# Grouped 5x5 convolutions on TensorE: from sixteen 32x32 tiles to eight 64x32 tiles, with the image rows read back from DRAM

## The chip, the cores and the metric

The kernel runs on one core of a Trainium2 chip. The core has TensorE (PE, matrix products), VectorE (DVE), ScalarE (ACT), GpSimd (POOL) and SyncE (SP); DMAs are issued by SP and POOL. The metric is the time of one execution on the device in microseconds, and lower is better. All numbers are f32.

## The reference, cut to what matters

The input is 4 images of 512 channels and 64x64 pixels. The first layer is a linear attention. It projects the image to queries, keys and values; a second set of them comes from a 5x5 depthwise convolution of the first set, followed by a pointwise convolution inside groups of 8 channels:

```python
qkv = concat(h @ wq.T, h @ wk.T, h @ wv.T)                        # 3 x 512 channels
dw  = conv(qkv, dw_kernel, 5x5, SAME, feature_group_count=3*512)  # each channel by itself
pw  = conv(dw, pw_kernel, 1x1, feature_group_count=3*64)          # 8 channels to 8
f   = concat(qkv, pw)                                             # 128 heads of 8
query, key = relu(...), relu(...)
scores = einsum("bhdn,bhen->bhde", value_with_ones, key)
out = einsum("bhde,bhen->bhdn", scores, query); out = out[:-1] / (out[-1:] + 1e-15)
x = batchnorm(conv1x1(out)) + x
```

The second layer computes four edge maps from the result (3x3 stencils), takes them through 1x1 convolutions, a channel attention, a fusing product with a layer norm, and adds the input.

## The kernel before, in words

The kernel computes the two convolutions of keys and queries (5x5 by channel, then 8 to 8) as one. The weights `mat` are made on POOL as products of the depthwise and pointwise weights (`load_mat`, L242 to L252, loaded as `dp_sb`). For values the kernel does not convolve; it correlates turned keys with shifted values instead (`correlate`, L457).

The 512 channels of each image are worked on in 4 groups of 128, so 16 groups in all. An image of 64 rows is cut into eight strips of 8 rows: strip j = (half, k) has the rows 32 half + k + 4 n, so every fourth row. `project` (L268) makes one strip of keys or queries: four matmuls of 128x128 weights and 512 columns, a copy to `strip` on ACT (L277), and then four DMAs from POOL (L283), each with 32 channels. They put the strip into a kept tile `inps[t]` of four row phases: partition 4 c + r holds channel c and the rows with phase r, so that 32 partitions are 8 channels by 4 rows.

`convolve` (L402) contracts those 32 partitions: 8 channels and 4 neighbouring rows at once. Its 32 output columns are 4 rows by 8 channels. Since 4 output rows need 8 input rows, each output takes two blocks `b` of four rows, and five column shifts `dx`. There are 16 tiles of 32x32 (four row quadrants i, four column quadrants j), so 5 x 2 x 16 = 160 matmuls into four PSUM banks. ACT copies the banks out with a relu (L415 for keys, L421 for queries).

What PE does is an order written out by hand. `keys_and_values` (L563 and on) projects a group's keys and values, strip by strip, and between them does the end of the group before: its queries' convolutions, divisions and foldings. `queries` projects the queries and convolves the keys. After the first image, the later layers of the image before (`stages`: `project_out` L661, `edge_branches` L738, `fuse_out` L850) lie between these steps: `run` and `advance` give them a share of the time after every step, by planned times such as `T_CONV`. The other engines and the SP queue are ordered by a scheduler, with priorities in the order of the program.

SP issues nearly all loads and stores: x (L259), weights (L240), the value strips `vt` to DRAM (L303) and back as `near` (L442), the divided heads and cheads (L390, L559), and for the later layers `hd` (L643, L645), `xr` (L658), `win`, `yr` and `ef`. POOL issues the strips (L283), `y` (L670) and `ef` (L751).

Of the kernel before, what the change touches and what calls it, by code (L numbers as in the profile page):

```python
# [8 lines left out]
F32 = mybir.dt.float32  # L9
# [65 lines left out]

LEFT_E = 14.0

T_PROJ, T_TURN, T_SCORES, T_CONV, T_CORR, T_SMALL = 3.4, 0.5, 0.3, 10.6, 1.1, 0.9


WORK, VALS = 18, 3
# [8 lines left out]
def conv_seq_kernel(  # L90
# [13 lines left out]
    gw = front.enter_context(tc.tile_pool(name="gw", bufs=2))  # L104
    vals = front.enter_context(tc.tile_pool(name="vals", bufs=VALS))
    work = front.enter_context(tc.tile_pool(name="work", bufs=WORK))
    ctx.enter_context(tc.manual_schedule(engines={mybir.EngineType.PE}))

    def work_tile(name, n=512):
# [12 lines left out]
    def rows(ap, width=W):  # L122
        return ap.rearrange("p (r c) -> p r c", c=width)
# [18 lines left out]
    nc.gpsimd.memset(ones, 1.0)  # L142


    inps = {}
    for t in (KEY, QUERY):
        inps[t] = keep.tile([P, 4, NB, W], F32, name=f"inp{t}")
        nc.gpsimd.memset(inps[t][:, :, 0, :], 0.0)
        nc.gpsimd.memset(inps[t][:, :, NB - 1, :], 0.0)

    vts = []
    for n in range(3):
# [73 lines left out]
    class Group:  # L226


        def __init__(self, b, heads, cheads, folded, g):
            self.b, self.heads, self.cheads, self.folded, self.g = b, heads, cheads, folded, g  # L230
            self.near_dram = near[(NG * b + g) % 2]
            self.w, self.mat = {}, {}
            self.strip, self.rq, self.held, self.conv, self.near = {}, {}, {}, {}, {}
            self.nears = iter([(half, jp, b) for half in range(2) for jp in range(2) for b in range(2)])


# [4 lines left out]

        def load_mat(self, t):  # L242

            dp = gw.tile([P, 4, 48], F32, name="dp_sb", tag="dp_sb", bufs=2)
            nc.sync.dma_start(out=dp, in_=dpk[self.g, t // QUERY])
            self.mat[t] = gw.tile([P, 4, 40, 8], F32, name="mat", tag="mat")
            nc.gpsimd.tensor_tensor(
                self.mat[t],
                dp[:, :, 0:40].unsqueeze(3).to_broadcast([P, 4, 40, 8]),
                dp[:, :, 40:48].unsqueeze(2).to_broadcast([P, 4, 40, 8]),  # L250
                ALU.mult,
            )  # L252

# [8 lines left out]
        def project(self, t, j):  # L262
            half, k = STRIPS[j]
            if (self.b, j) not in xs:
                self.load_x(j)
            ps = ps_tile("proj")
            for c in range(NCH):
                nc.tensor.matmul(  # L268
                    ps, lhsT=self.w[t][:, c, :], rhs=xs[self.b, j][c], start=(c == 0), stop=(c == NCH - 1)
                )  # L270
# [6 lines left out]
            nc.scalar.copy(s, ps)  # L277
            if t == KEY:
                self.strip[j] = s

            r, b = (k + 2) % 4, 8 * half + (k + 2) // 4
            for n in range(4):
                nc.gpsimd.dma_start(out=inps[t][r::4, n, b : b + 8, :], in_=rows(s)[32 * n : 32 * n + 32, :, :])  # L283

        def values(self, j):
            half, k = STRIPS[j]
# [106 lines left out]

        def convolve(self, t, half):
            banks = quad_tiles("cv")
            last = len(DXS) * 2 - 1
            for n, (dx, b) in enumerate((dx, b) for dx in DXS for b in range(2)):
                c0, c1 = _span(dx, W)
                for j in range(4):
                    for i in range(4):  # L400
                        q = slice(32 * i, 32 * i + 32)
                        nc.tensor.matmul(  # L402
                            rows(banks[i])[32 * j : 32 * j + 32, :, c0:c1],
                            lhsT=self.mat[t][q, j, (dx + 2) * 8 + 4 * b : (dx + 2) * 8 + 4 * b + 4, :],
                            rhs=inps[t][q, j, 8 * half + b : 8 * half + b + 8, c0 + dx : c1 + dx],
                            start=(n == 0), stop=(n == last),
                        )
# [155 lines left out]
        def keys_and_values(self, before):  # L563
# [16 lines left out]
            def co(jp, first):  # L580
# [5 lines left out]
                q("convolve", QUERY, 0), pj(KEY, 4), q("mix"), q("conv_weights"), sc(2), tr(3), pj(VALUE, 4),  # L586
                q("conv_heads"), q("conv_denominators", 0), pj(KEY, 5), q("conv_fold"), sc(3), tr(4), q("conv_divide", 0),
                pj(VALUE, 5), q("convolve", QUERY, 1), pj(KEY, 6), sc(4), tr(5), pj(VALUE, 6), q("conv_denominators", 1),
                [(0.0, self.load_wtab)], pj(KEY, 7), sc(5), tr(6), q("conv_divide", 1), pj(VALUE, 7),
                [(0.0, lambda: self.load_near(VALS))],  # L590
            ], [])

        def queries(self):


            def pj(j):
                return [(T_PROJ, lambda: self.project(QUERY, Q_ORDER[j]))]
# [366 lines left out]
    for n, cur in enumerate(groups):  # L964
        cur.load_mat(KEY)
        cur.load_w(QUERY)
        if n < 2:
            near_border(near[n])
        run(cur.keys_and_values(groups[n - 1] if n else None))
        if n and n % NG == 0:  # L970
            last = groups[n - 1]
# [152 lines left out]
```

## Time and profile before

| | |
|---|---|
| three runs | 4884.3, 4897.24, 4912.68 us; median 4897.24 |
| profiled execution | span 4886.7 us, from the first to the last instruction; no other time of it is given; clock granted to PE 0.979 |
| PE | 4653.5 us busy (95%) |
| DVE, ACT, POOL | 2103.5, 1593.8, 1113.0 us busy (43%, 33%, 23%) |
| DMA | 864.11 MB, 177 GB/s; the queue of SP 49.0%, that of POOL 9.0% of 16 engines' time |

The profile has a row for each group of equal instructions: source line, engine, operation, output and inputs, shape, count, then after a bar the busy time in us and the mean of one in ns, and after another bar the engine's idle time just before them with what ended most of it. An f32 matmul gives two records, each with a weight load. Matmuls are pipelined, so the mean of one record (600 ns) is longer than the time by which the next follows; busy time counts overlapping records once. Views of a single stretch list an engine's instructions in order of time, merged where they are alike.

### The profile page before, as it was taken

What the parts mean: (1) busy time and instruction counts of PE and PEld (TensorE: products, weight loads), DVE (VectorE), ACT (ScalarE), POOL (GpSimd) and SP (SyncE); (2) the same over time, 40 slices, a digit from 0 to 9 for tenths busy, and PEclk for the clock granted to TensorE, in tenths of its full rate; (3) what the DMA queues carried; (4) which work ended last, traced back from release to release, by engine and by line L of the source; (5) the groups of instructions that cost most, each with busy time, mean ns of one, the idle gap of its engine ahead of it and who ended that gap; (6) DMA issues with size and microseconds to landing.
All of it is one profiled execution on the core that took longest, in us unless ns stands there. A gap on an engine that the chain in (4) does not pass through costs nothing. (4 is left out here: it accounts for less than half of the span.)

```text
span 4886.7 us, 107506 instructions
## 1 busy us (share of the span) xinstructions
PE 4653.5 (95%) x46140; PEld 2698.7 (55%) x46140; DVE 2103.5 (43%) x2788; ACT 1593.8 (33%) x2725; POOL 1113.0 (23%) x1535
## 2 busy tenths in 40 slices
PE   9999999999999999999999999989999999799987
PEld 5666655455666565454565666445446566444433
DVE  1222222114555635311365553441125666447966
ACT  2121111002454524300244452430013545214765
POOL 3122212111221214311212121431111211011443
PEclk9999999999999999999999999999999999899998
DMA  6444456665665666766565666666556555564445
GB/s 205 133 129 134 135 191 188 163 173 162 205 185 188 196 204 202 223 181 161 175 189 191 183 201 186 203 200 192 152 169 184 184 181 185 160 166 148 152 144 170
DMA packets 469227, 864.11 MB, mean 177 GB/s; under 512 B 193000, under 2 KB 225800, under 8 KB 450320
## 3 DMA queue, kind: packets, MB, share of 16 engines
q1 hardware_dynamic: 415760, 721.90, 49.0%
q0 software_dynamic: 52992, 135.35, 9.0%
q8 instruction: 363, 5.95, 0.5%
q14 instruction: 112, 0.92, 0.1%
HBM read 575.93 MB, written 213.98 MB: 162 GB/s over the span
## 5 line engine op out<-in xcount | busy, mean ns | idle before, releaser
L268 PE MATMUL proj<-xt,w_sb 128*128 128x512 f32 x2048 | 942.3, 603 | 32.3 <-DMA xt<-in_x 27.5
L661 PE MATMUL yps<-hd,fold_sb 128*128 128x512 f32 x2048 | 903.5, 597 | 14.7 <-DMA hd<-heads 13.2
L283 POOL DMA_DIRECT2D inp<-strip x1024 | 546.4, 536 | 1345.4 <-ACT strip L277 1314.2
L402 PE MATMUL cv<-inp,mat 32*32 32x512 f32 (+1 forms) x20480 | 738.7, 600 | 60.0 <-issue 43.1
L661 PEld LDWEIGHTS yps<-hd,fold_sb 128*128 128x128 f32 x2048 | 385.5, 191 | 504.2 <-issue 463.8
L268 PEld LDWEIGHTS proj<-xt,w_sb 128*128 128x128 f32 x2048 | 377.9, 192 | 513.4 <-issue 450.8
L402 PEld LDWEIGHTS cv<-inp,mat 32*32 32x32 f32 x20480 | 448.3, 104 | 319.0 <-issue 160.8
L850 PE MATMUL zps<-ef,wf_sb 128*128 128x512 f32 (+1 forms) x1056 | 470.3, 599 | 29.6 <-ACT z L855 15.7
L290 PEld LDWEIGHTS val<-w_sb,xt 128*128 128x128 f32 x4096 | 471.1, 192 | 42.0 <-issue 32.8
L290 PE MATMUL val<-w_sb,xt 128*128 128x128 f32 x4096 | 486.6, 277 | 0.0
L738 PE MATMUL br<-maps,wbr_sb 128*128 128x256 f32 (+1 forms) x1792 | 464.7, 412 | 0.6 <-issue 0.4
L666 DVE SCALAR_TENSOR_TENSOR yt<-yps,shift,xr 128x512 f32<-128x512 f32 x128 | 96.0, 750 | 820.4 <-PE yps L661 790.4
L738 PEld LDWEIGHTS br<-maps,wbr_sb 128*128 128x128 f32 x1792 | 335.2, 190 | 138.2 <-issue 97.3
L277 ACT COPY strip<-proj 128x512 f32<-128x512 f32 x256 | 148.9, 582 | 653.8 <-PE proj L268 653.8
L850 PEld LDWEIGHTS zps<-ef,wf_sb 128*128 128x128 f32 x1056 | 204.1, 197 | 273.6 <-issue 230.3
L457 PE MATMUL corr<-near,ckt 128*32 128x160 f32 x8192 | 330.9, 314 | 21.3 <-DMA near<-near 21.3
L714 DVE TENSOR_TENSOR maps<-dv 128x1054 f32<-128x1054 f32 (+1 forms) x112 | 159.6, 1425 | 396.4 <-PE br L738 396.3
L670 POOL DMA_DIRECT2D y<-yt x128 | 114.7, 896 | 945.4 <-DVE yt L666 772.2
L457 PEld LDWEIGHTS corr<-near,ckt 128*32 128x32 f32 x8192 | 255.3, 111 | 115.9 <-issue 60.0
L881 POOL TENSOR_TENSOR z<-z,yr 128x512 f32<-128x512 f32 (+1 forms) x132 | 174.9, 1343 | 223.0 <-ACT z L878 125.2
L751 POOL DMA_DIRECT2D ef<-ef_o x112 | 81.8, 730 | 613.6 <-ACT ef_o L746 587.6
L318 ACT ACTIVATE kt<-tr 128x512 f32<-128x512 f32 x128 | 76.1, 595 | 438.5 <-PE tr L316 437.9
(131 smaller groups left out, 4373.3 us busy)
## 6 DMA issues: line engine op xcount, KB each, us to landing
xt<-in_x SPq DMA_DIRECT2D x316, 512.0 KB
near<-near SPq DMA_DIRECT2D x512, 264.0 KB
inp<-strip POOLq DMA_DIRECT2D x1024, 64.0 KB, 3.7
win<-y SPq DMA_DIRECT2D x96, 396.0 KB
near<-vt SPq DMA_DIRECT2D x512, 66.0 KB
y<-yt POOLq DMA_DIRECT2D x128, 264.0 KB, 6.3
heads<-q SPq DMA_DIRECT2D x128, 256.0 KB
cheads<-cq SPq DMA_DIRECT2D x128, 256.0 KB
```

The source lines that it names most:

```text
L268: nc.tensor.matmul(ps, lhsT=self.w[t][:, c, :], rhs=xs[self.b, j][c], start=(c == 0), stop=(c == NCH - 1))
L277: nc.scalar.copy(s, ps)
L283: nc.gpsimd.dma_start(out=inps[t][r::4, n, b : b + 8, :], in_=rows(s)[32 * n : 32 * n + 32, :, :])
L290: nc.tensor.matmul(ps[:, ts(c, P)], lhsT=xs[self.b, j][n][:, ts(c, P)], rhs=self.w[VALUE][:, n, :], start=(n == 0), stop=(n == NCH - 1),)
L402: nc.tensor.matmul(rows(banks[i])[32 * j : 32 * j + 32, :, c0:c1], lhsT=self.mat[t][q, j, (dx + 2) * 8 + 4 * b : (dx + 2) * 8 + 4 * b + 4, :],
L457: nc.tensor.matmul(self.banks[jj][32 * i : 32 * i + 32, 160 * b : 160 * b + 160], lhsT=self.held["c", i][:, at : at + 32], rhs=v[:, 4 * n ...
L661: nc.tensor.matmul(ps, lhsT=fold_sb[g // NG][:, g % NG, ts(c, P)], rhs=hd[g], start=(g == 0), stop=(g == 2 * NG - 1),)
L670: nc.gpsimd.dma_start(out=y[c, :, at : at + 29 : 4, :], in_=yt)
L714: nc.vector.tensor_sub(flat[:, half : 3 * half - 2], dvs[:, 2 : 2 * half], dvs[:, 0 : 2 * half - 2])
L738: nc.tensor.matmul(rows(ps), lhsT=wbr_sb[:, k, c, :], rhs=rows(maps[:, slot[k], c % 2, :], WB)[:, :, 0:W], start=(c == 0), stop=(c == NCH ...
L850: nc.tensor.matmul(ps, lhsT=wf_sb[:, k, ts(c, P)], rhs=ef[k], start=(k == 0), stop=(k == 3))
L881: nc.gpsimd.tensor_add(rows(z), rows(z), rows(yr, WB)[:, :, 1 : W + 1])
```

## The change

The kept tiles `inps` go. Each strip is stored whole, by one POOL DMA, into a DRAM tile `flat` (phase, channel, row, column; two of them for keys and two for queries, used in turn by the groups). Its two border rows are zeroed once. A new method `roll` reads one half of the image back, by eight SP DMAs, into a tile `rolled` whose partition 8 c + r holds channel c and eight neighbouring rows r of each block of four. Every row is read twice, as one of the first four and as one of the last four. 64 partitions are now 8 channels by 8 rows, so a convolution contracts all rows an output needs at once and has no `b` any more: 5 shifts x 2 sets s x 4 column quadrants j x 2 row halves i = 80 matmuls on 64x32 tiles. Set s = 0 fills the first two banks, set s = 1 the other two. Weights are laid out anew for that, with as many elements. The rolls of the keys are issued at the end of `keys_and_values`, those of the queries at the end of `queries`. The planned `T_CONV` changes from 10.6 to 9.2.

```diff
-T_PROJ, T_TURN, T_SCORES, T_CONV, T_CORR, T_SMALL = 3.4, 0.5, 0.3, 10.6, 1.1, 0.9
+T_PROJ, T_TURN, T_SCORES, T_CONV, T_CORR, T_SMALL = 3.4, 0.5, 0.3, 9.2, 1.1, 0.9
...
+    rolled = front.enter_context(tc.tile_pool(name="rolled", bufs=2))
...
-    inps = {}
-    for t in (KEY, QUERY):
-        inps[t] = keep.tile([P, 4, NB, W], F32, name=f"inp{t}")
-        nc.gpsimd.memset(inps[t][:, :, 0, :], 0.0)
-        nc.gpsimd.memset(inps[t][:, :, NB - 1, :], 0.0)
+    flats = {
+        (t, n): dram.tile([4, P, NB, W], F32, name=f"flat{t}{n}", bufs=1) for t in (KEY, QUERY) for n in range(2)
+    }
+    def flat_border(n):
+        for t in (KEY, QUERY):
+            for r in range(4):
+                nc.gpsimd.dma_start(out=flats[t, n][r, :, 0 if r < 2 else NB - 1, :], in_=zero_row[:, 0, 0:W])
...
-            for n in range(4):
-                nc.gpsimd.dma_start(out=inps[t][r::4, n, b : b + 8, :], in_=rows(s)[32 * n : 32 * n + 32, :, :])
+            nc.gpsimd.dma_start(out=self.flat[t][r, :, b : b + 8, :], in_=rows(s))
+        def roll(self, t, half):
+            self.rolled[t, half] = rolled.tile([P, 8, 512], F32, name="rolled", tag="rolled")
+            for r in range(8):
+                at = 8 * half + r // 4
+                nc.sync.dma_start(
+                    out=self.rolled[t, half][r::8, :, :],
+                    in_=self.flat[t][r % 4, :, at : at + 8, :].rearrange("(n c) b w -> c n (b w)", c=16),
+                )
...
         def convolve(self, t, half):
             banks = quad_tiles("cv")
-            last = len(DXS) * 2 - 1
-            for n, (dx, b) in enumerate((dx, b) for dx in DXS for b in range(2)):
-                c0, c1 = _span(dx, W)
-                for j in range(4):
-                    for i in range(4):
-                        q = slice(32 * i, 32 * i + 32)
-                        nc.tensor.matmul(
-                            rows(banks[i])[32 * j : 32 * j + 32, :, c0:c1],
-                            lhsT=self.mat[t][q, j, (dx + 2) * 8 + 4 * b : (dx + 2) * 8 + 4 * b + 4, :],
-                            rhs=inps[t][q, j, 8 * half + b : 8 * half + b + 8, c0 + dx : c1 + dx],
-                            start=(n == 0), stop=(n == last),
-                        )
+            image = self.rolled.pop((t, half))
+            for s in range(2):
+                for n, dx in enumerate(DXS):
+                    c0, c1 = _span(dx, W)
+                    for j in range(4):
+                        for i in range(2):
+                            q = slice(64 * i, 64 * i + 64)
+                            nc.tensor.matmul(
+                                rows(banks[2 * s + i])[32 * j : 32 * j + 32, :, c0:c1],
+                                lhsT=self.mat[t][q, 4 * s + j, (dx + 2) * 4 : (dx + 2) * 4 + 4, :],
+                                rhs=rows(image[q, 2 * j + s, :])[:, :, c0 + dx : c1 + dx],
+                                start=(n == 0), stop=(n == len(DXS) - 1),
+                            )
...
# keys_and_values:
-                [(0.0, self.load_wtab)], pj(KEY, 7), sc(5), tr(6), q("conv_divide", 1), pj(VALUE, 7),
-                [(0.0, lambda: self.load_near(VALS))],
+                [(0.0, self.load_wtab)], pj(KEY, 7), sc(5), tr(6), [(0.0, lambda: self.roll(KEY, 0))],
+                q("conv_divide", 1), pj(VALUE, 7),
+                [(0.0, lambda: self.load_near(VALS)), (0.0, lambda: self.roll(KEY, 1))],
...
# queries:
-                ct(1, 3), own("denominators", 0),
+                [(0.0, lambda: self.roll(QUERY, 0)), (0.0, lambda: self.roll(QUERY, 1))], ct(1, 3), own("denominators", 0),
```

More of the change, by code (lines that the diff above doesn't have):

```diff
@@ L232, in __init__ @@
             self.w, self.mat = {}, {}
-            self.strip, self.rq, self.held, self.conv, self.near = {}, {}, {}, {}, {}
+            self.strip, self.rq, self.held, self.conv, self.near, self.rolled = {}, {}, {}, {}, {}, {}
+            self.flat = {t: flats[t, (NG * b + g) % 2] for t in (KEY, QUERY)}
             self.nears = iter([(half, jp, b) for half in range(2) for jp in range(2) for b in range(2)])
@@ L242, in load_mat @@
         def load_mat(self, t):
-            dp = gw.tile([P, 4, 48], F32, name="dp_sb", tag="dp_sb", bufs=2)
+            dp = gw.tile([P, 8, 28], F32, name="dp_sb", tag="dp_sb", bufs=2)
             nc.sync.dma_start(out=dp, in_=dpk[self.g, t // QUERY])
-            self.mat[t] = gw.tile([P, 4, 40, 8], F32, name="mat", tag="mat")
+            self.mat[t] = gw.tile([P, 8, 20, 8], F32, name="mat", tag="mat")
             nc.gpsimd.tensor_tensor(
                 self.mat[t],
-                dp[:, :, 0:40].unsqueeze(3).to_broadcast([P, 4, 40, 8]),
-                dp[:, :, 40:48].unsqueeze(2).to_broadcast([P, 4, 40, 8]),
+                dp[:, :, 0:20].unsqueeze(3).to_broadcast([P, 8, 20, 8]),
+                dp[:, :, 20:28].unsqueeze(2).to_broadcast([P, 8, 20, 8]),
                 ALU.mult,
@@ L968, in conv_seq_kernel @@
             near_border(near[n])
+            flat_border(n)
         run(cur.keys_and_values(groups[n - 1] if n else None))
@@ L1046 @@
     dw = a["L0_conv_dw_kernel"].reshape(3 * C, 5, 5)[order].reshape(NG, 3, 4, 4, 8, 5, 5)
-    dwk = np.zeros((NG, 3, 4, 8, 4, 4, 5, 8), dw.dtype)
-    for r in range(4):
-        for k in range(8):
-            if 0 <= k - 3 + r < 5:
-                dwk[:, :, :, :, r, :, :, k] = dw[:, :, :, :, :, k - 3 + r, :].transpose(0, 1, 3, 4, 2, 5)
-    dwk = dwk.reshape(NG, 3, P, 4, 40)[:, [KEY, QUERY]]
+    split = dw.reshape(NG, 3, 4, 2, 2, 8, 5, 5).transpose(0, 1, 4, 5, 3, 2, 7, 6)
+    dwk = np.zeros((NG, 3, 2, 8, 8, 2, 4, 5, 4), dw.dtype)
+    for r in range(8):
+        for m in range(4):
+            if 0 <= r + m - 3 < 5:
+                dwk[:, :, :, :, r, :, :, :, m] = split[..., r + m - 3]
+    dwk = dwk.reshape(NG, 3, P, 8, 20)[:, [KEY, QUERY]]
     pw = a["L0_conv_pw_kernel"].reshape(3 * C, 8)[order].reshape(NG, 3, 4, 4, 8, 8)
-    pwk = pw.transpose(0, 1, 3, 5, 2, 4)[:, [KEY, QUERY]]
-    pwk = np.broadcast_to(pwk[:, :, :, :, None], (NG, 2, 4, 8, 4, 4, 8))
-    pwk = pwk.reshape(NG, 2, P, 4, 8)
+    pwk = pw.reshape(NG, 3, 4, 2, 2, 8, 8).transpose(0, 1, 4, 6, 3, 2, 5)[:, [KEY, QUERY]]
+    pwk = np.broadcast_to(pwk[:, :, :, :, None], (NG, 2, 2, 8, 8, 2, 4, 8))
+    pwk = pwk.reshape(NG, 2, P, 8, 8)
     dpk = np.concatenate([dwk, pwk], axis=4)
```

## The prediction

> **What bounds the kernel now.** I read the page first: the busy shares, then the costliest groups, then the queues.
>
> ```profile
> PE 4653.5 (95%) x46140; PEld 2698.7 (55%) x46140; DVE 2103.5 (43%) x2788; ACT 1593.8 (33%) x2725; POOL 1113.0 (23%) x1535
> ...
> L283 POOL DMA_DIRECT2D inp<-strip x1024 | 546.4, 536 | 1345.4 <-ACT strip L277 1314.2
> L402 PE MATMUL cv<-inp,mat 32*32 32x512 f32 (+1 forms) x20480 | 738.7, 600 | 60.0 <-issue 43.1
> ```
>
> TensorE (PE) is busy for 95% of the span and runs in one written order, so its time is the kernel's time until another resource makes it wait. L402 is the convolutions: 64 of them (4 in each of 16 groups), 320 records each, two for every f32 matmul. Busy plus idle before them is 738.7 + 60.0 = 798.7 us, or 12.48 us for one. Of the idle time, "issue" is time in which PE waited for nothing that the profile shows.
>
> Then I read PE's order of time around three convolutions: one without a hole, and two with.
>
> ```profile
> 2527.94 10.64 PE L402 MATMUL cv<-inp,mat 32*32 32x512 f32 x320
> 2538.51 1.98 PE L268 MATMUL proj<-xt,w_sb 128*128 128x512 f32 x4
> ...
> 2609.63 4.56 PE L402 MATMUL cv<-inp,mat 32*32 32x512 f32 x126
> 2617.40 6.47 PE L402 MATMUL cv<-inp,mat 32*32 32x496 f32 x194 [3.20 <-issue]
> 2623.80 2.43 PE L738 MATMUL br<-maps,wbr_sb 128*128 128x256 f32 x10
> ...
> 479.46 2.27 PE L402 MATMUL cv<-inp,mat 32*32 32x496 f32 x48
> 483.23 6.32 PE L402 MATMUL cv<-inp,mat 32*32 32x504 f32 x176 [1.50 <-issue]
> ```
>
> The columns are start, length, instruction, count, and in brackets the idle time before. The undisturbed one takes 2538.51 - 2527.94 = 10.57 us to the next work. The second takes 2623.80 - 2609.63 = 14.17 us; 3.20 of the difference is one hole inside the convolution. The queues say what the hole may be:
>
> ```profile
> q1 hardware_dynamic: 415760, 721.90, 49.0%
> q0 software_dynamic: 52992, 135.35, 9.0%
> q8 instruction: 363, 5.95, 0.5%
> ```
>
> Queue 8 carries instructions: 5.95 MB in 363 packets, 16.4 KB each. PE has 2 x 46140 = 92280 instructions in busy records; shared out, that is 64 B each and some 256 to a packet. A convolution of 640 instructions eats a packet's worth every 10.57 x 256 / 640 = 4.2 us, faster than other long stages: a projection's 16 take 3.6 us. Read packet by packet, the trace has one that starts at 2044.4 inside a further hole of 2.94 us that ends at 2047.05. So the excess over 10.57 us is mostly late instructions.
>
> **Part 1: the shape of the matmuls.** The new convolution has 80 matmuls on 8 tiles of 64x32, the old one 160 on 16 tiles of 32x32. Per tile nothing changes: ten matmuls of 64, 63 or 62 columns by 8 rows (502 on average), one after another. So streaming alone gives no gain; the gain is in what lies between. One old step (16 matmuls, one on each tile) takes 10.57 / 10 = 1.057 us. L661's chain advances 903.5 / 2048 = 0.441 us per record of 512 columns, so a step's two records stream for 2 x 0.441 x 502 / 512 = 0.866 us, and 0.191 us per step is lost. The other row with column tiles is L457, correlations on four tiles of 128x32 with 160 columns:
>
> ```profile
> L457 PE MATMUL corr<-near,ckt 128*32 128x160 f32 x8192 | 330.9, 314 | 21.3 <-DMA near<-near 21.3
> L457 PEld LDWEIGHTS corr<-near,ckt 128*32 128x32 f32 x8192 | 255.3, 111 | 115.9 <-issue 60.0
> ```
>
> A step of its four tiles is 8 records, 8 x 330.9 / 8192 = 0.323 us by this row, and 0.306 in the undisturbed stretches (4.89 us for 128 records). Streaming is 2 x 0.441 x 160 / 512 = 0.276, so 0.03 to 0.05 us is lost. No row has 8 tiles. If the loss is like that of four tiles, a convolution takes 10 x (0.866 + 0.038) = 9.04 us; if it grows in proportion between 4 and 16 tiles, 0.038 + 0.153 x 4/12 = 0.089, it takes 9.55. I take 9.2. The outer bounds are 8.7 (nothing lost) and 10.57 (lost as now).
>
> A rule speaks against this part. The Trainium skill, "TensorE: Matmul & The Clock Gate", Part 3, says that weight loads overlap matmuls in flight only where the row group differs; the change leaves two row groups of four. By it the step would lose at least what it loses now, and the sum below would end near 4827. L457 works with one row group, all 128 rows, and its loads of 111 ns lie almost entirely under the matmuls, so I weigh the row more.
>
> **Part 2: half the instructions.** Leaving out the idle time that other engines cause at L402 (DVE's weighed tiles 13.6 and cq 3.2 us, which I leave as they are), the convolutions cost 798.7 - 16.8 = 781.9 us. Of that 64 x 10.57 = 676.5 is the undisturbed time, and 105.4 is excess. Now 320 instructions would last 9.2 us, so 256 of them last 7.4 instead of 4.2 us. A late packet has 3.2 us more in hand, and the longest holes are little longer than that. I leave 10 us of the excess; the bounds are 0 and 60. Where the skill differs, it would take this term away: "Runtime: NRT & Kernel Launch", Instruction fetch mechanics, calls the crossing of a 16 KiB boundary mostly hidden. In this trace the convolutions show 43.1 us of "issue" idle, which is not hidden.
>
> The shorter convolution covers less of other engines' work; but its first two banks are now complete at half time, so ACT's copies start some 4.6 us earlier, which is as much as is lost: 0. T_CONV only spreads the background work anew: 0.
>
> Together: 64 x 9.2 = 588.8, plus 10 = 598.8, against 781.9: **-183 us**.
>
> **Part 3: the strips, on POOL.** Gone are 1024 issues of 536 ns (549 us of POOL), come are 256 stores of a whole strip. The nearest rows are the 256 KB stores L751 at 730 ns and L670 at 896 ns, so 187 to 229 us. POOL is idle for 77% and is no path: 0. A strip is now in DRAM about 3.9 us after issue (the landing of L751's), against 3.7 for the last of four. The border rows are 16 small issues near the start, beside the first loads; the memsets that go were some 0.3 us each: 0. The weight tables keep their 1280 elements per partition: 0.
>
> **Part 4: the rolls, on SP and its queue.** 64 rolls of 8 DMAs of 256 KB are added, 2.10 MB each, 134 MB in all. Queue 1 now moves 721.9 MB in 49.0% of 16 x 4886.7 us, so a roll takes all 16 engines 2.10 / 721.9 x 0.49 x 4886.7 = 7.0 us, and all rolls 445 us: the queues' share goes from 58% to 67%. No ceiling. SP needs 8 issues of 0.33 (hd) to 0.645 us (near), 2.6 to 5.2 us per roll.
>
> Are they in time? Two buffers hold the rolls, so each waits for the convolution two before it, which in PE's order always stands well ahead of its issue. The rolls of the queries have 28 us or more until their convolution. The first roll of the keys has least, from the last key projection to the convolution:
>
> ```profile
> 414.27 3.70 PE L268 MATMUL proj<-xt,w_sb 128*128 128x512 f32 x8
> ...
> 428.03 3.60 PE L268 MATMUL proj<-xt,w_sb 128*128 128x512 f32 x8
> 431.56 10.71 PE L402 MATMUL cv<-inp,mat 32*32 32x512 f32 x320
> ```
>
> and SP's order in that time:
>
> ```profile
> 418.00 0.34 SPq L240 DMA_DIRECT2D w_sb<-in_wqkv  x1
> 420.81 2.71 SPq L559 DMA_DIRECT2D cheads<-cq  x4
> ```
>
> The projection ends at 417.97, the convolution starts at 431.56: 13.6 us. The roll's rows of half 0 come from strips 0 to 5, written before, and SP has a hole from 418.3 to 420.8. Issue 5.2, data 7.0 (overlapping) and a landing of some 2 us end near 427: in time. If the roll waits for strip 7 too (copy 0.6, issue 0.7, landing 3.9), it ends near 5.2 + 7.0 + 3.7 = 15.9 us after the projection, 2.3 late; with six such groups, 14 us.
>
> Behind the rolls on SP and in queue 1 stand cheads stores, weights, vt stores, and loads of x, heads and windows. PE now waits 63.3 us on DMAs (x 27.5, near 21.3, heads and cheads 14.5). In proportion to load that is +10; an upper bound of 90 is one full roll before an urgent load in each of the 12 groups with other work beside them (84 us) and some. Below nothing there is no gain to be had from more traffic. I take 10 + 14, **+25 us**.
>
> **Sum.** The profiled execution spans 4886.7 us, no other time of it is given; the median of three runs is 4897.24, 10.5 above and inside their range. 4897.2 - 183 + 25 = 4739; I say 4738.
>
> **The rivals.**
>
> *The step keeps its loss.* Two row groups hide weight loads no better than four. Then only the late instructions go: 4897.2 - 95 + 25 = 4827. For it: the loss per step could be one of tiling in rows, which L457 has not. 0.14.
>
> *SP's order makes PE wait: slower.* SP issues in order, and one delay now costs PE much (SP's order of time, then PE's):
>
> ```profile
> 3296.26 0.47 SPq L259 DMA_DIRECT2D xt<-in_x  x1
> ```
>
> ```profile
> 3302.34 3.38 PE L268 MATMUL proj<-xt,w_sb 128*128 128x512 f32 x4 [21.71 <-DMA xt<-in_x]
> ```
>
> The load of x was issued behind other transfers that had waited, and PE stood for 21.7 us. If the 4 MB of query rolls, or the first key roll waiting on its strip, cause one such stall in each of the 12 groups with other work, that is 260 us: 4897 - 183 + 260 = 4974. It decides from (183 + 24.5) / 21.7, ten such stalls. Against it: the trace has one in 16 groups. 0.11.
>
> *The traffic eats the gain.* 160 to 207 us of DMA waits, 36 to 47% of the rolls' 445 us, leave the time as it was. 0.05.
>
> **Numbers.** The forecast has 0.70. Faster by over 0.5% (24.5 us, about what a measurement of this kernel can tell) are it and the first rival: 0.84; same 0.05; slower 0.11. Range: the low end is 8.9 us per convolution, no late instructions and no DMA cost: 4897 - 212 = 4685, and below that 15 us for run to run, 4670. The high end takes in the first rival with 20 us more, 4850.
>
> **What would show it.** L402's successor has 10240 records, busy plus idle near 605 us, undisturbed ones of 9.0 to 9.55 us; 10.5 would mean the first rival. Queue 8 shrinks by 64 x 320 x 64 B = 1.3 MB, and holes inside convolutions nearly vanish. Queue 1 moves 856 MB. PE's waits on x, near and heads stay under 100 us; over 250 the prediction is wrong. A wait of the key convolution on the rolls of over 2 us each would show the late strip.

## The result, and the profile after

The changed kernel takes 5192.5 us (median of four runs, 5191.7 to 5196.2) against 4897.3 for the one before on the same chip: the ratio is 1.061, with a 95% interval from 1.058 to 1.064. It is 6% slower where 3% faster was predicted. The profiled execution spans 5189.9 us, and the clock granted to PE is 0.938 instead of 0.979.

The page of the changed kernel: busy shares, queues, and the rows that answer to those of before (count, then busy and mean ns, then idle time before and what ended it).

```profile
PE 4546.4 (88%) x35900; PEld 2470.7 (48%) x35900; DVE 2106.5 (41%) x2788; ACT 1613.6 (31%) x2735; POOL 717.8 (14%) x779
...
q1 hardware_dynamic: 489488, 856.68, 58.4%
q0 software_dynamic: 41216, 135.82, 8.0%
q8 instruction: 283, 4.64, 0.4%
...
L274 PE MATMUL proj<-xt,w_sb 128*128 128x512 f32 x2048 | 992.3, 629 | 366.9 <-DMA xt<-in_x 359.4
...
L418 PE MATMUL cv<-rolled,mat 64*32 64x504 f32 (+2 forms) x10240 | 563.3, 587 | 13.4 <-DVE weighed L491 10.5
...
L288 POOL DMA_DIRECT2D flat<-strip x256 | 141.9, 554 | 1917.3 <-ACT strip L283 1731.2
```

The convolutions did what was hoped, and more: busy plus idle is 563.3 + 13.4 = 576.7 us instead of 798.7. Not one of them waited long for its roll; the idle time that is left there is DVE's. But PE is busy for 88% only, and the projections (L274) now wait 359.4 us for x, where they waited 27.5. PE's order of time shows an undisturbed convolution (start, length, instruction, count, idle before):

```profile
2524.21 8.65 PE L418 MATMUL cv<-rolled,mat 64*32 64x512 f32 x160
2532.80 3.70 PE L274 MATMUL proj<-xt,w_sb 128*128 128x512 f32 x8
```

From its start to that of the next work are 2532.80 - 2524.21 = 8.59 us, against 10.57; 54 of the 64 are within 0.3 us of that.

The waits of PE itself, total, number and longest, say where the time went:

```profile
PE proj L274 <- DMA xt<-in_x: 359.4, 26, 42.0
PE yps L678 <- DMA hd<-heads: 44.4, 8, 13.9
PE zps L867 <- DMA ef<-ef: 38.2, 3, 26.1
```

So do those of SP, the engine that issues x, heads and rolls alike; L295 is the roll:

```profile
SPq L295 <- DMA flat<-strip: 319.1, 40, 18.7
...
SPq L295 <- DMA near<-near: 162.2, 102, 4.0
...
SPq L265 <- DMA rolled<-flat: 33.0, 40, 1.1
```

SP stands before its rolls until strips have landed in DRAM (319.1 us), and before rolls and other loads until earlier, unrelated DMAs of its own have landed (the other two rows, and many small ones). The second kind is a matter of eight places. In the trace, SP's DMAs go round eight semaphores in turn, 2697 DMAs before and 3209 after without an exception, and each is issued only when the DMA eight before it has landed. I counted the time from SP's last issue to that landing wherever the next issue follows it within 0.3 us: 155 us before, 505 us after.

One such stall, first in SP's order of time, then in PE's:

```profile
777.01 17.07 SPq L295 DMA_DIRECT2D rolled<-flat  x8
794.75 1.54 SPq L246 DMA_DIRECT2D w_sb<-in_wqkv  x2
797.12 0.33 SPq L645 DMA_DIRECT2D fold_sb<-folded  x1
798.12 1.59 SPq L660 DMA_DIRECT2D hd<-heads  x2
800.54 4.03 SPq L662 DMA_DIRECT2D hd<-cheads  x4
804.62 15.76 SPq L265 DMA_DIRECT2D xt<-in_x  x6
```

```profile
816.66 5.07 PE L274 MATMUL proj<-xt,w_sb 128*128 128x512 f32 x8 [32.70 <-DMA xt<-in_x]
```

Eight roll DMAs, some 4.8 us of issuing (594 ns each), hold SP for 17.07 us. What they wait for here are not strips: eight near loads had just been issued, and SP's waits in the stretch from 770 to 825 us name them for 12.5 us.

```profile
SPq L295 <- DMA near<-near: 12.5, 6, 4.0
```

Loads that had been due stand behind the rolls, x last, and PE stands for 32.70 us.

Put together from PE's busy and idle times, the span grew by 303 us like this: convolutions -222, all other waits of PE +458, and +68 because PE's other work ran more slowly (the projections alone 50); that is 304, to 1 us.

### The profile page after: what moved, and what is told of

It reads as the page before. It is cut to its first block, busy times and chain, and to the rows that moved or that the text cites. A ratio compares the mean times of both kernels' runs of the same rounds, so it can differ in the third digit from the quotient of the medians.

```text
span 5189.9 us, 86329 instructions
## 1 busy us (share of the span) xinstructions
PE 4546.4 (88%) x35900; PEld 2470.7 (48%) x35900; DVE 2106.5 (41%) x2788; ACT 1613.6 (31%) x2735; POOL 717.8 (14%) x779
## 3 DMA queue, kind: packets, MB, share of 16 engines
q1 hardware_dynamic: 489488, 856.68, 58.4%
q8 instruction: 283, 4.64, 0.4%
## 5 line engine op out<-in xcount | busy, mean ns | idle before, releaser
L274 PE MATMUL proj<-xt,w_sb 128*128 128x512 f32 x2048 | 992.3, 629 | 366.9 <-DMA xt<-in_x 359.4
L678 PE MATMUL yps<-hd,fold_sb 128*128 128x512 f32 x2048 | 907.0, 599 | 48.7 <-DMA hd<-heads 44.4
L274 PEld LDWEIGHTS proj<-xt,w_sb 128*128 128x128 f32 x2048 | 393.9, 201 | 882.3 <-issue 718.4
L418 PE MATMUL cv<-rolled,mat 64*32 64x504 f32 (+2 forms) x10240 | 563.3, 587 | 13.4 <-DVE weighed L491 10.5
L288 POOL DMA_DIRECT2D flat<-strip x256 | 141.9, 554 | 1917.3 <-ACT strip L283 1731.2
L418 PEld LDWEIGHTS cv<-rolled,mat 64*32 64x32 f32 x10240 | 190.9, 107 | 354.7 <-issue 326.7
L281 ACT ACTIVATE rq<-proj 128x512 f32<-128x512 f32 x128 | 76.1, 595 | 516.7 <-PE proj L274 505.8
L724 DVE TENSOR_TENSOR dv<-win 128x528 f32<-128x528 f32 (+1 forms) x112 | 90.4, 807 | 330.6 <-DMA win<-y 325.1
```

The source lines that it names most:

```text
L274: nc.tensor.matmul(ps, lhsT=self.w[t][:, c, :], rhs=xs[self.b, j][c], start=(c == 0), stop=(c == NCH - 1))
L288: nc.gpsimd.dma_start(out=self.flat[t][r, :, b : b + 8, :], in_=rows(s))
L418: nc.tensor.matmul(rows(banks[2 * s + i])[32 * j : 32 * j + 32, :, c0:c1], lhsT=self.mat[t][q, 4 * s + j, (dx + 2) * 4 : (dx + 2) * 4 + 4, :],
L678: nc.tensor.matmul(ps, lhsT=fold_sb[g // NG][:, g % NG, ts(c, P)], rhs=hd[g], start=(g == 0), stop=(g == 2 * NG - 1),)
```

## The experiments

My theory after the result: the matmul side is worth what was predicted, and the rolls cost more because they stand in SP's order. Rivals: the rolls' bytes fill the queues whoever issues them; or a 64x32 step gains less than it seems. The kernel before took 4872 to 4897 us on the chips used, so each run is compared with the runs of before beside it. Without any rolls the kernel is 192.2 us faster than before, and what is called the cost of a variant is its difference to before plus 192. The changed kernel's cost is 295.3 + 192.2 = 487 us. Single runs have no interval; differences under 20 us say nothing.

### The matmuls alone

Two kernels have no rolls; the convolutions read two tiles of zeros. The second also cuts every matmul of the convolutions into two with half the columns, so that the instructions are 640 again and the streaming stays the same.

```diff
-            self.rolled[t, half] = rolled.tile([P, 8, 512], F32, name="rolled", tag="rolled")
-            for r in range(8):
...
+            self.rolled[t, half] = kept[half]
```

```diff
-            for s in range(2):
+            for s, u in ((0, 0), (0, 4), (1, 0), (1, 4)):
...
-                                rhs=rows(image[q, 2 * j + s, :])[:, :, c0 + dx : c1 + dx],
+                                rhs=rows(image[q, 2 * j + s, :])[:, u : u + 4, c0 + dx : c1 + dx],
```

Without rolls: 

> No rolls at all: the convolutions read two kept tiles of zeros, strips are stored to DRAM as in the change and never read back. It leaves out the input of the convolutions. Both theories: the pure worth of the new shape; convolutions at 8.95 us each save 222 us against before, PE's waits on DMAs are those of before, so 4660 to 4720 us. Over 4800 would mean that the rolls are not the cause.

With halved matmuls: 

> No rolls, as in d_noroll (4680 us), and each of the 80 matmuls of a convolution is cut into two of 256 columns, so that a convolution has the 640 instructions of before on the new tiles. It leaves out the input of the convolutions. If the excess of before over its undisturbed convolutions (105 us) was late instructions: 9.2 to 9.5 us undisturbed, 256 instructions in 3.8 us, holes of issue inside the convolutions again, and 4800 us or more. If the excess came with the old tiles: only the undisturbed time grows, and the time is 4690 to 4730 us.

Measured: 4680.1 us without rolls (before: 4872.3), and 4772.3 with halved matmuls (before: 4874.9). The rows of the convolutions on the page, first without rolls, then halved:

```profile
L416 PE MATMUL cv<-kept,mat 64*32 64x504 f32 (+2 forms) x10240 | 560.0, 585 | 8.5 <-DVE weighed L489 5.4 <-DVE cq L572 3.1
```

```profile
L416 PE MATMUL cv<-kept,mat 64*32 64x252 f32 (+2 forms) x20480 | 606.6, 380 | 81.5 <-issue 74.0 <-DVE weighed L489 3.8 <-DVE cq L572 3.0
```

What follows: the matmul side is worth 192 us. With the instructions doubled, 74.0 us of "issue" are back and the queue of instructions carries 5.93 MB again; the fastest halved convolution takes 8.63 us, as long as the fastest whole one (8.58), but the mean one 10.64. So the extra instructions cost nothing by their streaming. By coming late they add 120 us to the convolutions (606.6 + 81.5 against 560.0 + 8.5) and 90 to the kernel, since PE waits less elsewhere. That the holes are late instructions can be read from the packets of queue 8: all 48 holes of "issue" in the halved convolutions end 1.15 to 1.60 us after such a packet has landed, and so do all 33 in the kernel before (43.1 us). Of random moments in the convolutions, fewer than one in ten would.

### Is it the bytes, the strips, or SP?

The same rolls issued by POOL; the rolls on SP from a DRAM tile `still` of zeros, so that nothing waits for strips; and both at once.

```diff
-                nc.sync.dma_start(
+                nc.gpsimd.dma_start(
                     out=self.rolled[t, half][r::8, :, :],
```

```diff
-                    in_=self.flat[t][r % 4, :, at : at + 8, :].rearrange("(n c) b w -> c n (b w)", c=16),
+                    in_=still[r % 4, :, at : at + 8, :].rearrange("(n c) b w -> c n (b w)", c=16),
```

POOL: 

> The rolls are issued by POOL instead of SP; nothing else is changed. Order theory (SP, in order, stands before a roll whose strip has not landed, and the loads of x behind it come late; the profile after has PE waiting 359 us on x, against 28 before): SP never waits for a strip, PE's wait on x falls under 100 us and the time to 4700 to 4850 us. Traffic theory (134 MB more are moved by the same 16 engines, whoever issues them): PE still waits over 250 us on DMAs and the time stays over 5050 us.

SP, no strips: 

> The rolls stay on SP but read a zeroed DRAM tile that no strip writes, so they wait for no strip; the same 2 MB each are moved, and strips are still stored. The convolutions are computed from zeros, so this leaves out their result. Order theory: with no strips to wait for, SP is free and the time is 4700 to 4900 us. Traffic theory: over 5050 us. If the rolls, no longer held by strips, are put early and wait for their buffer instead, SP's wait at the roll names the convolution, and the time lies between.

POOL, no strips: 

> Rolls on POOL, as in a_pool (4829 us), reading a zeroed DRAM tile that no strip writes. It leaves out the input of the convolutions. a_pool is 149 us slower than d_noroll. If that is POOL standing for its own strips: 4690 to 4750 us. If it is the traffic itself, which slows the near loads: 4800 to 4840 us.

Measured: POOL 4828.7 us, ratio 0.991 (0.989 to 0.993), a cost of 149, as the order theory said. SP without strips 5160.1, a cost of 480, as much as with them: the order theory as it stood, with strips as the reason why SP stands, missed. POOL without strips 4808.9, a cost of 126. On POOL the same 512 DMAs, and PE's wait for x, read like this:

```profile
L295 POOL DMA_DIRECT2D rolled<-flat x512 | 272.4, 536 | 694.4 <-PE cv L418 348.5 <-DMA flat<-strip 261.6 <-issue 29.8
...
PE proj L274 <- DMA xt<-in_x: 34.0, 8, 5.2
```

POOL stands 694 us before them and nobody minds, since PE's loads are not behind them. On SP without strips, its waits at the rolls are for earlier DMAs and, for 63.5 us, for the convolution that frees the buffer, and PE's wait for x stays:

```profile
SPq L304 <- DMA near<-near: 265.6, 163, 3.2
SPq L304 <- PE cv L427: 63.5, 17, 11.2
SPq L304 <- DMA rolled<-still: 50.7, 80, 1.3
...
PE proj L283 <- DMA xt<-in_x: 318.4, 24, 40.6
```

Its order of time, then PE's, has the same kind of stall as with strips:

```profile
1473.55 2.59 SPq L327 DMA_DIRECT2D near<-vt  x4
1476.18 4.91 SPq L467 DMA_DIRECT2D near<-near  x7
1481.19 14.32 SPq L304 DMA_DIRECT2D rolled<-still  x8
1496.54 1.63 SPq L255 DMA_DIRECT2D w_sb<-in_wqkv  x2
1499.08 1.24 SPq L718 DMA_DIRECT2D win<-y  x2
1501.14 4.54 SPq L274 DMA_DIRECT2D xt<-in_x  x5
```

```profile
1509.39 5.98 PE L283 MATMUL proj<-xt,w_sb 128*128 128x512 f32 x7 [16.71 <-DMA xt<-in_x]
```

Seven near loads of 264 KB had taken seven of the eight places. In the window from 1476 to 1510 us five of the roll DMAs waited for a near load to land, 9.7 us in all and 3.1 at most. What follows: bytes alone cost about 126 us, and that SP issues them costs the rest. "The strips come late", my first idea of why SP stands, is not needed for it.

### Can the order be mended?

Five kernels move something in the order. Rolls queued behind later stores, so that they come when their strips have landed, the queries' rolls moved into the next group (on SP, then on POOL); on POOL, the second key roll after the first key convolution; x loaded by POOL, with the rolls still on SP; and, without rolls, x loads queued behind the last value store but one. That puts all 78 loads of x for key strips behind that store, where 47 are in the changed kernel and 21 were before (of a strip's two loads, the second is counted here and below).

```diff
+            with tc.issue_after(stored[-1]):
+                for r in range(8):
...
```

```diff
-                nc.sync.dma_start(out=xt, in_=x[self.b, j, :, 2 * n : 2 * n + 2, :])
+                nc.gpsimd.dma_start(out=xt, in_=x[self.b, j, :, 2 * n : 2 * n + 2, :])
```

SP, behind value stores: 

> The rolls stay on SP, with their strips as source, but each is queued behind a store of values that SP issues after its strips have landed (keys behind the stores of the values 6 and 7, queries behind those of values 0 and 1 of the next group). Order theory: SP's waits for strips (319 us) nearly vanish and the time falls to 4720 to 4900 us. Traffic theory: 64 bursts of 2 MB still stand ahead of the loads in the same queue, over 5050 us.

POOL, behind strip stores: 

> Rolls on POOL, those of the queries moved into the next group as in f_after, each queued behind a store of strips on POOL. If the wait of near loads (57 us of PE in a_pool) comes from the query rolls that run beside them at the end of a group: 4740 to 4800 us. If the cost is the traffic wherever it lies: 4810 to 4850 us.

POOL, second key roll later: 

> Rolls on POOL as in a_pool (4829 us), the second key roll moved behind the first key convolution, so that it does not run beside the near loads at the end of the keys. If near's 57 us of PE time come from that overlap: under 25 us and 4770 to 4810 us. If they come from the query rolls or from the traffic at large: 4815 to 4840 us.

x on POOL: 

> The change with rolls on SP as they are, and the loads of x moved to POOL instead. If the loss is x standing behind rolls in SP's order: PE's wait on x falls from 359 to under 80 us and the time to 4780 to 4880 us. If the other loads behind the rolls (heads, windows, near, ef) cost as much: 4900 to 5000 us. If it is the traffic alone: over 5050 us, and PE waits for x as long as before.

x late, no rolls: 

> No rolls (d_noroll, 4680 us), but from the second image on each load of x is queued behind the last but one store of values, as 47 of 78 key loads are in the change against 21 of 78 before. It leaves out the input of the convolutions. If the order that the scheduler gave SP is a cause by itself, without the rolls' bytes and waits: PE's wait on x is over 150 us and the time over 4830 us. If only rolls in the way make x late: 4680 to 4740 us.

Here `stored[-1]` is the last value store for SP, and the last strip store for POOL. Measured: SP behind value stores 5003.2 us, ratio 1.027 (1.024 to 1.029), cost 323. That lies between the two ranges: SP's waits for strips fell from 319.1 to 17.1 us, and two thirds of the cost stayed. POOL behind strip stores 5024.4, ratio 1.030 (1.027 to 1.032): a miss, 193 us worse than POOL without that, and unexplained. POOL with the second key roll later 4852.2, ratio 0.991 (0.988 to 0.995), with the same wait for near (57.9 us against 57.0): a miss too, that wait does not come from the place of that roll. x on POOL 5176.4, ratio 1.058 (1.055 to 1.062), cost 475. x late without rolls 4715.4, a cost of 14 us (35 if the two times are compared directly): the order alone is not the cause. PE's waits with x on POOL:

```profile
PE br L755 <- ACT maps L741: 129.7, 11, 26.6
PE br L755 <- DVE maps L746: 79.7, 4, 26.5
PE corr L473 <- DMA near<-near: 51.2, 10, 9.9
PE corr L473 <- DMA xr<-in_x: 48.1, 1, 48.1
PE zps L867 <- DMA ef<-ef: 43.6, 3, 24.9
```

The wait for x is down to 12.2 us and the time is nearly the same, in the range that was expected for traffic alone, with x as late as before. But the windows, near, xr and ef still stand behind the rolls, and the windows, for which DVE waits 236.6 us, make ACT and DVE late with the maps. To rescue one load from SP's order only shows the next.

### What it is in SP's order

By then I held that SP's standing was the cost, since the runs above agreed with a cost of 0.44 to 0.49 of the time that SP stood before and in its roll DMAs, beyond what the bytes cost (0.42 to 0.50 with the costs as given here). Two kernels with two tiles of zeros for the convolutions tried it: one keeps four of the eight DMAs of each roll, the other issues eight DMAs of a few bytes each with the same strip waits.

```diff
+            self.rolled[t, half] = kept[half]
             for r in range(8):
                 at = 8 * half + r // 4
                 nc.sync.dma_start(
...
+                    out=rows(kept[half][r::8, 0, :])[:, :, 0:1],
+                    in_=self.flat[t][r % 4, 0:16, at : at + 8, 0:1],
                 )
```

Four of eight: 

> d_noroll with half of the rolls back on SP: four of the eight DMAs, the rows 0 to 3 of each block, 1 MB a roll. The other rows stay zero, so the convolutions lack them. The full rolls on SP cost 512 us over d_noroll. Queue theory (SP's order is the order of transfers, and a burst holds SP for the time of its bytes; the first microseconds are hidden by loads that are made ahead): less than half, 4750 to 4900 us. If each roll cost by the waits for its strips alone: half or more of 512 us, over 4930 us.

Eight tiny ones: 

> The convolutions read two tiles of zeros, as in the run without rolls, and for every roll eight DMAs of a few bytes are issued by SP, each reading the strips that the roll's DMA would read: the same places in SP's order and the same waits on the strips, but no traffic (the convolutions' values are not computed). If SP's order is what costs, because SP stands before the strips and everything behind stands with it, the cost over the run without rolls (4680) is 0.44 to 0.49 of the time that SP stands at and issues these DMAs (868 us with the full rolls, perhaps 600 to 850 here): 4930 to 5090, with the wait on x above 200 us. If it is the bytes of the rolls, before other loads on the queue, that costs: 4690 to 4740, with the wait on x under 60. In between, 4800 to 4900, would say that the strip waits are prolonged by the bytes themselves.

Measured: four of eight 4959.8 us, cost 277, in the range for strip waits alone; eight tiny ones 4745.8, cost 53, 6 us above the range for the bytes. The waits of SP, then of PE, with the tiny ones:

```profile
SPq L299 <- DMA flat<-strip: 435.0, 78, 18.8
```

```profile
PE proj L278 <- DMA xt<-in_x: 66.2, 9, 23.3
```

This felled that theory. SP stands 435.0 us before strips, longer than in the changed kernel, and spends as long at its roll DMAs (831 us with the issues, 868 there), and PE's wait for x is 66.2 us instead of 359.4. It is neither the strips nor the issues by themselves, nor, by the runs on POOL, the bytes by themselves; and so the range that four of eight fell into does not speak for strip waits either.

What is left is that bytes and the eight places multiply: a roll of eight DMAs takes all places, so that SP can't issue what follows until 256 KB after 256 KB has landed. Then fewer, larger DMAs must help with not one byte less. The next two runs test that: two DMAs of 1 MB per roll from the zeros; and POOL's rolls from zeros together with the tiny DMAs and strip waits on SP.

```diff
-            for r in range(8):
...
+            for r in range(2):
                 nc.sync.dma_start(
...
+                    out=self.rolled[t, half][64 * r : 64 * r + 64, :, :],
+                    in_=still.rearrange("r p b w -> (r p) (b w)")[:, 0:512].rearrange("(c n) f -> c n f", n=8),
```

Two DMAs, no strips: 

> SP's rolls read a DRAM tile of zeros without any wait on strips, as in the run that cost 480 us over the run without rolls (4680), but a roll is 2 DMAs of 1 MB instead of 8 of 256 KB: the same 2.1 MB per roll in packets of 2048 bytes, 128 issues instead of 512 (the convolutions' values are not computed). If the eight places of SP count (each DMA of SP waits until the one eight before has landed), a roll takes two places instead of all eight and the loads behind it are issued at once: cost 150 to 300, 4830 to 4980, wait on x under 150 us. If the bytes of the rolls ahead in the queue hold the loads back, nothing changes: cost 420 to 520, 5100 to 5200, wait on x near 320 us.

Bytes on POOL, waits on SP: 

> The rolls' bytes go by POOL's queue from a DRAM tile of zeros (alone 4809, 129 us over the run without rolls), and SP issues eight DMAs of a few bytes per roll that wait for the strips (alone 4746, 66 us over it); the convolutions' values are not computed. If bytes and strip waits cost much only where both stand in SP's order, the two add up: 4840 to 4920. If SP's standing before strips is costly as soon as the queues are as full as in the changed kernel, whichever queue carries the bytes: over 5000.

Measured: two DMAs 4821.4 us, cost 133 against 480 for eight, with the same 856.65 MB on the queue and no less time of the 16 DMA engines (62.9% of 4819.2 us, that is 3031, against 57.6% of 5158.3, that is 2971). It is even less than the 150 to 300 expected. Bytes on POOL and waits on SP 4865.2, cost 177, the sum of 126 and 53 to 2 us. PE's wait for x with two DMAs:

```profile
PE proj L283 <- DMA xt<-in_x: 108.1, 13, 19.6
```

The scheduler put the x loads at much the same places as with eight: 37 of 78 loads for key strips stand ahead of the value store two strips before, against 32. What differs is how long SP waits for a place: 199 us instead of 603.

### Fewer DMAs with the strip waits

The changed kernel with two DMAs per roll (the same strips read, but laid down in another arrangement, which leaves out the convolutions' result); and the whole change with another order of partitions and strips in DRAM, (channel half, row group, channel, row), in which a roll is four DMAs of 512 KB, on SP and on POOL.

```diff
+            for i in range(2):
+                for u in range(2):
+                    at = 8 * half + u
+                    nc.sync.dma_start(
+                        out=self.rolled[t, half][64 * i + 32 * u : 64 * i + 32 * u + 32, :, :],
+                        in_=self.flat[t][8 * i : 8 * i + 8, :, :, at : at + 8, :].rearrange("c r n b w -> (c r) n (b w)"),
+                    )
```

Two, with strips: 

> The changed kernel with a roll of 2 DMAs of 1 MB on SP instead of 8 of 256 KB, the same strips read and waited for and the same bytes, but laid in another order over the partitions (the convolutions' values are wrong). If the eight places are the cause and the strip waits add what they added without bytes (66), the cost over the run without rolls is about 141 + 66: 4840 to 4940. If bytes and strip waits together in SP's order cost more than their sum, whatever the places: 5000 to 5150, as half the bytes in 4 DMAs (280) would suggest.

Four on SP: 

> The whole change with another order of the partitions, (channel half, row group, channel, row), and of the strips in DRAM, so that a roll is 4 DMAs of 512 KB on SP: four of the eight places per roll. By the places the cost lies between those of 2 DMAs (141, and 66 for the strip waits) and of 8 (512): 4900 to 5050, ratio 1.00 to 1.035. If only the bytes and strip waits on SP count: as the changed kernel, 5150 to 5200, ratio 1.05 to 1.065.

Four on POOL: 

> The same with the 4 DMAs of a roll issued by POOL. POOL holds nothing that PE waits for soon, so the number of DMAs should matter little there: as with 8 DMAs on POOL (4829, ratio 0.991), 4800 to 4840, ratio 0.984 to 0.994. Under 4780 would say that POOL's places or its issues cost there as well.

Measured: two 4954.9 us, 15 above the range for the places; four on SP 5055.9, ratio 1.037 (1.035 to 1.039), 6 above its range; four on POOL 4875.2, ratio 1.000 (0.999 to 1.001). PE's waits for x, with two and with four on SP:

```profile
PE proj L274 <- DMA xt<-in_x: 204.1, 14, 39.3
...
PE proj L277 <- DMA xt<-in_x: 243.2, 18, 40.7
```

The runs on SP side by side, all in us; the fourth column is my count from the trace described above, the last the mean time from an x load's buffer coming free to its issue (the second of each strip's two loads, some 150 in the later images):

| rolls on SP | strip waits | cost | waits for a place | x load issued after |
|---|---|---|---|---|
| none | no | 0 | 131 | 1.7 |
| 8 tiny | yes | 53 | 162 | 3.3 |
| 2 of 1 MB | no | 133 | 199 | 3.2 |
| 2 of 1 MB | yes | 270 | 290 | 4.6 |
| 4 of 512 KB | yes | 371 | 384 | 6.2 |
| 8 of 256 KB | no | 480 | 603 | 9.3 |
| 8 of 256 KB (the change) | yes | 487 | 505 | 9.6 |

At equal bytes and equal strip waits, the cost rises with the number of DMAs: 270, 371, 487. The waits for a place are not the cost by themselves: with eight on POOL they are 314 us at a cost of 149. It matters what stands behind them. And no run changes the number of places itself, so that it is the places by which fewer, larger DMAs help is argued from the last two columns, not shown by itself.

Four on POOL missed what was expected: it is 41 us worse than eight on POOL, its strip stores are in more packets and SP waits 449 us for places against 314. Why, I have not settled; some of the 371 of four on SP may have the same source.

## Why the prediction was wrong

**Parts 1 and 2 held, in part by luck.** -183 us was predicted for the matmuls and 192 measured without rolls. On the profiles the convolutions saved 230 (798.7 to 560.0 + 8.5), and PE's other waits, which the prediction put at 0, took 22 back (153.0 to 174.6); the kernel before also ran some 16 us faster on that chip than in its profile (4870.5 against 4886.7). Within them, the undisturbed convolution takes 8.58 us where 9.2 was taken and 8.7 was the outer bound: a step takes 0.858 us where streaming alone was reckoned at 0.866, so eight tiles lose nothing. The first rival, that a step keeps its loss, is refuted. So is, for this case, what was drawn from the rule weighed against the change (the Trainium skill, "TensorE: Matmul & The Clock Gate", Part 3): with two row groups the weight loads of 107 ns add nothing to the step. Nor was the old loss one of the number of instructions, since the halved matmuls issue as many as before and take 8.63 us undisturbed. That late instructions were the excess is shown by the same run. The Trainium skill, "Runtime: NRT & Kernel Launch", Instruction fetch mechanics, calls such crossings mostly hidden; here 48 of some 160 in the halved convolutions (40960 instructions, 256 to a packet) left a hole, 74.0 us in all. The queue of instructions fell by 5.95 - 4.64 = 1.31 MB, as reckoned.

**Part 4 failed.** Its +25 us measured 487. Three of its terms were wrong, and one question.

The term "in proportion to load +10" is the bytes: on POOL, without strips, they cost 126 us, on SP in two DMAs 133. The rolls' 445 us of all engines' time were too few: queue 1 took 636 us more (58.4% of 5189.9 us less 49.0% of 4886.7). Nor is the higher load free of cost, as other transfers land later: the median near load 8.7 us after its issue with zeros on POOL, 7.1 without rolls.

The term "2.6 to 5.2 us per roll" on SP counted the issues. They take 4.75 us per roll, inside the bounds; with the idle time before them SP spends 13.6. That the next issue can wait for an earlier transfer, with eight under way at most, could have been read from the trace of before, in the semaphores of SP's DMAs, and was not looked for. It is the largest term, if the step from two DMAs per roll to eight is the places': with strip waits, 487 - 270 = 217 us.

"Are they in time?" asked after the wrong victim. The convolutions never waited for their rolls, as reckoned. But the issues stood in SP's order ahead of x, heads, near and the windows, and the eight DMAs of a roll did not stand where the program has them: the scheduler spread them between other DMAs, some before their strips existed. Strip waits with the issues cost 53 us alone (14 were taken), and 270 - 133 - 53 = 84 more with the bytes. So 133 for bytes, 53, 84 and 217 make the 487; the split is of single runs, to some 20 us each and for the 84 to twice that.

**The second rival was the right one, and too cheap.** "SP's order makes PE wait" had the mechanism and the place, from the one stall of 21.7 us in the profile. It priced twelve stalls, 260 us, where there were 26 of x alone, 13.8 us on average; and it had no term for the other loads, nor for PE's slower work while it waits so often (+68 us). Its test was a good one: waits on x, near and heads were to stay under 100 us, over 250 the prediction is wrong, and 359.4 + 12.0 + 44.4 = 416 were measured. A chance of 0.11 came from "one in 16 groups" before, which says how much slack the order has without the rolls, not with them.

**The third rival**, that traffic eats the gain, needed 160 to 207 us of waits. The bytes alone cost less, 126 of a gain of 192, so traffic by itself would have left the change faster, as it does on POOL.

## What to carry to other kernels

A DMA added to a queue in order costs more than its bytes and its issue: count how many of the places for transfers under way it takes, and name what stands behind it. The same bytes cost 480 us in eight DMAs per roll and 133 in two, or 126 on a queue where nothing urgent stands behind. Try a faster step once with its new supply of data taken away: that one run splits the result into the part that works and the part that does not. The best version here is the change with the rolls on POOL, 0.991 (0.989 to 0.993) of the time before, a gain of 0.9% where 3% was predicted.

## What the runs showed of the hardware that was not expected

64x32 tiles stream without a measurable loss (0.858 us per step of eight matmuls), where 32x32 tiles lost 0.19 us per step of 16.

The mean granted clock goes down with PE's waits: 0.982 without rolls, 0.970 with the rolls on POOL and with two DMAs from zeros, 0.957 with two and strips, 0.946 with four, and 0.938 in the changed kernel. Most of that is waiting itself. In the changed kernel's clock records, 34 of PE's 35 waits of over 5 us end with the clock at half. It goes to half a median of 3.7 us after such a wait has begun and comes back 4.3 us after it has ended; of 58 waits under 2 us, 4 end so. Of the 642 us at half clock PE is busy for 231, against 131 of 205 before. Half of those 100 us more is lost, some 50 of the 68 us by which PE's other work ran more slowly.

An x load that PE waited for was late after its issue too: from its issue to the end of PE's stall the median is 9.3 us with eight DMAs from zeros and 9.4 in the changed kernel, against 4.6 and 6.1 in the two stalls before. The median of all x loads from issue to landing is 6.8 us in the changed kernel and 5.9 before.
